# A Mamba mixer on one NeuronCore: product with B to SBUF, scan and product with C in place, convolutions over shifted rows

## The chip, the cores and the metric

The kernel runs on one core of one Trainium2 chip. The metric is the device time of one execution in microseconds. Five engines work side by side, each with its instructions in order: TensorE (PE, with its weight loads PEld), VectorE (DVE), ScalarE (ACT), GpSimd (POOL) and SyncE (SP), which here issues nearly all DMAs. They wait for each other through semaphores.

## The reference, cut to what matters

The input is 8 sequences of 256 tokens with 128 features. A macaron of blocks runs over it; the last three are experts, mixer, experts, each added to the residual stream:

```python
x = x + 0.5 * ffn(layernorm(x)); x = x + attn(layernorm(x)); x = x + 0.5 * ffn(layernorm(x))
x = x + 0.5 * experts(layernorm(x))
x = x + mixer(layernorm(x))
x = x + 0.5 * experts(layernorm(x))
```

Only the mixer is touched. It projects to 256 channels x and 256 gates z, and runs one selective state-space branch forward and one over the reversed sequence:

```python
x = silu(causal_dwconv(x, conv_w, conv_b))            # 4 taps along the tokens
dt, Bm, Cm = split(einsum('bdl,ed->bel', x, xproj_w)) # 64, 16, 16
delta = softplus(dtproj_w @ dt + dt_bias)
dA  = exp(delta * A)                                  # 256 channels x 16 states
dBu = delta * Bm * x
h   = dA * h + dBu                                    # a recurrence over the 256 tokens
y   = (sum over states of h * Cm + D * x) * silu(z)
```

A third branch takes a 2-D FFT of x, a convolution of 5 taps, an inverse FFT and a normalized magnitude. The three are summed and projected back to 128 features.

## The kernel before

The first 1243 us hold the attention blocks and are the same in both kernels. Then `experts_and_mixer` runs. It works on 4 chunks of 512 tokens (two sequences each). The 256 channels x 16 states of a chunk are 32 *units* for the two directions `r`, the two channel halves `t`, four places `i` and two `jp`; a unit is a tile of 128 partitions (8 channels x 16 states) by 2 x 512 tokens. 4 x 32 = 128 units in all.

One loop over *slots* writes the order of TensorE, VectorE, ScalarE and GpSimd by hand (`tc.manual_schedule`); `at(slot, f, ...)` hangs other steps into a slot, ahead of the y-sums or, with `last=True`, behind them. In slot i:

- `scan(i)`: VectorE runs the recurrence (L1217, `tensor_tensor_scan`) over dA (SBUF) and pU (PSUM) into a tile h; then GpSimd multiplies h with C into a second tile hc (L1219).
- `feed(i + 1)`: VectorE multiplies pU by B, in place in PSUM (L1206).
- the steps of the slot; in odd slots `sums(i - 3)`, in which TensorE adds hc over the states into py (L1236).
- `spread(i + 2, m...)`, last in the slot: TensorE copies rows of `du` (delta times u) to the 128 partitions of a unit in pU (two PSUM tiles in turn), and rows of `dl` (delta) to p; ScalarE turns the latter into dA (L1197, L1199). After a *burst* of activation-table work the loop gives out no, one or two new dA a slot.

Steps that the change also touches: `convolve` (L1082) makes one direction of one half with 4 matmuls per output, one a tap, whose 128x128 weights `inK` are the projection times the tap (made on VectorE by `taps`, L872), so that the convolution is taken straight from the normalized features xT. `steps` (L1133) makes delta before the softplus, `delta` (L1153, L1155) adds its two terms on VectorE, multiplies by u on GpSimd and swaps the partition halves of du by two DMAs. `pairs` (L1267), `mirror`, `halves`, `folds` and `squares` are GpSimd's work on the FFT branch, `mix` (L1280), `over_channels` and `over_tokens` (L1312, L1313) TensorE's. `join` (L1416) sums the branches on GpSimd, `output` (L1425) projects, `add` (L1437) adds the residual on GpSimd. Expert tiles (`hidden` L1001 to L1010, `turn` L1019, `close` L1029) run in the slots before the first scan and, for the second block, after the last.

```python
dB = units[n]["dB"]
nc.vector.tensor_tensor(dB, dB, bcast(gots[ch]["B", r], 2), ALU.mult)
...
h = pool.tile([P, 2, CT], F32, tag="h", name="h", bufs=2)
...
nc.vector.tensor_tensor_scan(hf, af, bf, 0.0, ALU.mult, ALU.add)
st["hc"] = hc = pool.tile([P, 2, CT], F32, tag="hc", name="hc", bufs=4)
nc.gpsimd.tensor_tensor(hc, h, bcast(gots[ch]["C", r], 2), ALU.mult)
```

Of the kernel before, what the change touches and what calls it, by code (L numbers as in the profile page):

```python
# [17 lines left out]
P = 128  # L18
B, S, D = 8, 256, 128
CT = 512  # L20
# [795 lines left out]

def experts_and_mixer(nc, tc, ident, nhalf, x, cols, ins, w, given, store):
# [19 lines left out]
    with ExitStack() as ctx:  # L837
        pool = ctx.enter_context(tc.tile_pool(name="mamba", bufs=1))
        ps = psum(ctx, tc)

# [5 lines left out]
        xT = pool.tile([P, 2, S + 6], F32, name="xT")  # L846
        nc.gpsimd.memset(xT[:, :, 0:3], 0.0)
        nc.gpsimd.memset(xT[:, :, S + 3 :], 0.0)
        xTm = xT[:, :, 3 : S + 3]
# [4 lines left out]

        tiny = pool.tile([P, 1], F32, name="tiny")
# [5 lines left out]
        def at(slot, f, *a, last=False):  # L861
            (after if last else before).setdefault(slot, []).append(lambda: f(*a))
# [5 lines left out]

        def taps(r, t):

            to = w["inK"][:, r, t]
            nc.vector.tensor_tensor(to, to, bcast(w["inT"][:, t * P : (t + 1) * P], K), ALU.mult)  # L872
# [81 lines left out]
        class Experts:  # L954
# [39 lines left out]
            def hidden(self, n):  # L994
# [9 lines left out]
                h = pool.tile([P, 2, E, EH], F32, tag="h", name="hid", bufs=2)  # L1004
                gate = got["gate"][:, t : t + 1, :, :].to_broadcast([P, 2, E, EH])
                nc.vector.tensor_tensor(h, ph, gate, ALU.mult)  # L1006
                both = pool.tile([P, 2, 4, P], F32, tag="hc", name="sg_hT", bufs=4)
# [37 lines left out]
        def normalize(ch, part):  # L1045
            got = gots[ch]
            h = part % 2
            xh = x[ch][:, 2 * h : 2 * h + 2, :]
            if part < 2:
                got["stats", h] = ln_scales(nc, pool, nhalf, xh, 1e-5)  # L1050
                return
            if h == 0:
                got["xn"] = given["xT"].rearrange("p (t d) -> p t d", t=NT)
            ln_scaled(nc, xh, got["xn"][:, 2 * h : 2 * h + 2, :], got["stats", h])

        def features(ch):
            pt = bank([P, 2, S])
            for t in range(NT):
                nc.tensor.transpose(
                    pt[:, t // 2, t % 2 * P : (t % 2 + 1) * P], gots[ch]["xn"][:, t, :], ident  # L1060
                )
            nc.scalar.copy(xTm, pt)

        def gate(ch, t):
            got = gots[ch]
            if t == 0:
# [3 lines left out]
                pz, w["inT"][:, DI + t * P : DI + (t + 1) * P], xTm, start=True, stop=True  # L1070
            )
            nc.scalar.copy(got["sz"][:, t, :], pz.rearrange("p b l -> p (b l)"))

        def convolve(ch, t, r):
# [5 lines left out]
            for k in range(K):  # L1080
                o = k if r == 0 else 2 * (K - 1) - k
                nc.tensor.matmul(  # L1082
                    pu, w["inK"][:, r, t, k, :], xT[:, :, o : o + S], start=(k == 0), stop=(k == K - 1)
                )
# [20 lines left out]
        def ranks(ch, r):  # L1105

            got = gots[ch]
            if r == 0:
                got["low"] = pool.tile([LOW, 2, CT], F32, tag="low", name="low")
            px = bank([P, CT])[0:LOW, :]  # L1110
            for t in range(2):
                nc.tensor.matmul(  # L1112
                    px, w["xproj"][:, r, t, :], got["u", t][:, r, :], start=(t == 0), stop=(t == 1)
                )
            nc.scalar.copy(got["low"][:, r, :], px)

        def rows(ch, r, k):
# [4 lines left out]
            n = DR + DS * k  # L1122
# [3 lines left out]
        def steps(ch, t, r):  # L1126

            got = gots[ch]
            if r == 0:
                got["dl", t] = pool.tile([P, 2, CT], F32, tag=f"dl{t}", name=f"dl{t}")  # L1130
                got["ab"] = pool.tile([P, 2, CT], F32, tag="ab", name="ab")
            pd = bank([P, CT])
            nc.tensor.matmul(  # L1133
                pd,
                w["dtT"][:, r, t * P : (t + 1) * P],
                got["low"][0:DR, r, :],
                start=True,
                stop=True,
            )
            b = dt_b[:, r, t : t + 1]  # L1140
            nc.scalar.activation(got["ab"][:, r, :], pd, AF.Abs, bias=b)
            nc.scalar.activation(got["dl", t][:, r, :], pd, AF.Relu, bias=b)
# [6 lines left out]
        def delta(ch, t, part):  # L1149
# [5 lines left out]
            nc.gpsimd.tensor_tensor(ab, dl, u, ALU.mult)  # L1155

            du = pool.tile([P, 2, CT], F32, tag=f"du{t}", name=f"du{t}")
            nc.sync.dma_start(out=du[0:64], in_=ab[64:128])
            nc.sync.dma_start(out=du[64:128], in_=ab[0:64])
            got["du", t] = du  # L1160
# [14 lines left out]
        def spread(n, *ms):  # L1175
# [3 lines left out]
            if 0 <= n < N:  # L1179
                ch, t, r, i, jp = unit(n)  # L1180
                pU = ps.tile([P, 2, CT], F32, tag="u", name="pU")
                for jj in range(2):
                    todo.append((jj, pU[:, jj, :], gots[ch]["du", t][:, r, :], i, 2 * (1 - jp) + jj))
                units[n]["dB"] = pU
            ms = [m for m in ms if 0 <= m < N]
            decays = []
            for k, m in enumerate(ms):
                ch, t, r, i, jp = unit(m)
                dA = pool.tile([P, 2, CT], F32, tag="dA", name="dA", bufs=4)
                units[m]["dA"] = dA  # L1190
                for jj in range(2):
                    pA = bank([P, CT])
                    todo.append((2 * k + jj, pA, gots[ch]["dl", t][:, r, :], i, 2 * jp + jj))
                    decays.append((dA[:, jj, :], pA, A[:, r, t, i, 2 * jp + jj : 2 * jp + jj + 1]))
            for _, dst, src, i, j in sorted(todo, key=lambda v: v[0]):
                rs = slice(32 * j, 32 * j + 32)
                nc.tensor.matmul(dst, w["sel"][rs, i, :], src[rs, :], start=True, stop=True)  # L1197
            for dA, pA, rate in decays:
                nc.scalar.activation(dA, pA, AF.Exp, scale=rate)  # L1199

        def feed(n):
# [3 lines left out]
            dB = units[n]["dB"]  # L1205
            nc.vector.tensor_tensor(dB, dB, bcast(gots[ch]["B", r], 2), ALU.mult)  # L1206

        def scan(n):
# [4 lines left out]
            h = pool.tile([P, 2, CT], F32, tag="h", name="h", bufs=2)  # L1213
            hf, af, bf = (v.rearrange("p t l -> p (t l)") for v in (h, st["dA"], st["dB"]))
            if r == 1:
                hf, af, bf = (v[:, ::-1] for v in (hf, af, bf))
            nc.vector.tensor_tensor_scan(hf, af, bf, 0.0, ALU.mult, ALU.add)  # L1217
            st["hc"] = hc = pool.tile([P, 2, CT], F32, tag="hc", name="hc", bufs=4)
            nc.gpsimd.tensor_tensor(hc, h, bcast(gots[ch]["C", r], 2), ALU.mult)  # L1219

        def skip(ch, t, r):

            got = gots[ch]
            if r == 0:
                got["y", t] = ps.tile([P, CT], F32, tag="y", bufs=1, name="py")
            nc.tensor.matmul(  # L1226
                got["y", t], w["D"][:, 2 * r + t, :], got["u", t][:, r, :], start=(r == 0), stop=False
            )

        def sums(n):  # L1230
# [4 lines left out]
            for j in range(4):  # L1235
# [3 lines left out]
                    units[n + j // 2]["hc"][:, j % 2, :],  # L1239
                    start=False,  # L1240
                    stop=(n % 16 == 14),
                )
            units[n].clear()
# [15 lines left out]
        def pairs(ch, o):  # L1259
# [3 lines left out]
            if o == 1:  # L1263
                got["sd"] = pool.tile([P, 2, 2, 2, 2, M], F32, tag="f8", name="sd", bufs=2)
            lo, hi = (got["xe"][:, :, :, v : v + M] for v in (2 - o, 2 + o))
            for k, op in enumerate((ALU.add, ALU.subtract)):
                nc.gpsimd.tensor_tensor(got["sd"][:, k, o - 1], hi, lo, op)  # L1267
# [146 lines left out]
        def join(ch):  # L1414
            got = gots[ch]
            nc.gpsimd.tensor_tensor(  # L1416
                got["sz"], got["sz"], got["mag"].rearrange("p t b l -> p t (b l)"), ALU.add
            )

        def output(ch):  # L1420
            y = gots[ch]["sz"]
            po = bank([P, NT, D])
            for t in range(NT):
                for d in range(2):
                    nc.tensor.matmul(  # L1425
                        po[:, t, :],
                        y[:, d, t * P : (t + 1) * P],
                        w["outT"][:, d, :],
                        start=(d == 0),
                        stop=(d == 1),  # L1430
                    )
            o = pool.tile([P, NT, D], F32, tag="sq", name="o", bufs=2)
            nc.scalar.copy(o, po)
            gots[ch]["o"] = o

        def add(ch):
            nc.gpsimd.tensor_tensor(x[ch], x[ch], gots[ch]["o"], ALU.add)  # L1437
# [20 lines left out]
        for part, k in enumerate((-20, -18, -19, -17)):  # L1458
            at(k, normalize, 0, part)
        at(-16, features, 0)  # L1460
        for i in range(4):
            at(-15 + i, convolve, 0, 1 - i // 2, i % 2)
        at(-11, gate, 0, 0)
        at(-10, gate, 0, 1)
        at(-9, ranks, 0, 0)
# [4 lines left out]
        at(-13, silu, u_of(0, 1))  # L1470
        at(-11, silu, u_of(0, 0))
        at(-9, silu, sz_of(0))
# [22 lines left out]
        for i in range(4):  # L1495
            at(-23 + i, taps, i // 2, i % 2)
# [14 lines left out]
        bursts = set()  # L1511
        for ch in range(NCH):

            o = (ch - 1) * UNITS
            if ch == 0:
                at(-8, ranks, ch, 1)
                at(-8, largest, ch)
                at(-7, steps, ch, 0, 0)
                at(-6, steps, ch, 0, 1)
                at(-6, exponentials)  # L1520
                at(-6, softplus, ch)
            else:
                for part, k in enumerate((-23, -22, -1, -1)):
                    if ch == 1 and part < 2:
                        k = -6
                    at(o + (0 if ch == 1 and part > 1 else k), normalize, ch, part)
                at(o, features, ch, last=True)
                at(o + 2, convolve, ch, 1, 0)
                at(o + 6, convolve, ch, 1, 1)
                at(o + 8, convolve, ch, 0, 0)  # L1530
                at(o + 10, convolve, ch, 0, 1)
                at(o + 12, silu, u_of(ch, 1), u_of(ch, 0))
                at(o + 12, gate, ch, 0)
                at(o + 12, gate, ch, 1)
                at(o + 12, silu, sz_of(ch))
                at(o + 12, exponentials)
                at(o + 15, ranks, ch, 0)
                at(o + 16, ranks, ch, 1)
                at(o + 17, steps, ch, 0, 0)
# [341 lines left out]
```

## Time and profile before

| | us |
|---|---|
| median of 3 runs (lowest, highest) | 1970.21 (1969.56, 1971.91) |
| the profiled execution | 1971.64 |
| its span, first to last instruction | 1969.9 |
| busy in the span: PE, DVE, ACT, POOL | 1860.1, 1503.3, 1019.3, 1074.3 |
| first scan starts, last scan starts | 1352.8, 1896.9 |
| mean granted TensorE clock | 0.982 |

In the profile's rows a group is named by its source line, engine, operation and tiles (out<-in); after the count stand the busy time in us, the mean of one in ns, the engine's idle time just before these instructions, and what ended most of that. An instruction that has started and is held inside its engine counts as busy. TensorE's matmul times are modelled ends of pipelined work.

### The profile page before, as it was taken

The page shows a single profiled execution, that of the slowest core. Times are in us where ns is not written, and L with a number is a line of the kernel's source. Part 1 is how long each engine was busy: PE and PEld are TensorE (multiplying, and loading weights), DVE is VectorE, ACT ScalarE, POOL GpSimd, SP SyncE. Part 2 cuts the span into 40 slices and gives each one's busy share as a digit, 9 for nine tenths or more (in the row PEclk, how much of TensorE's full clock was granted, in tenths as well). Part 3 has the DMA queues.
Part 4 walks back from the last instruction along what each step waited for, and adds up shares of the span by engine and source line. Part 5 has one row for each costly group of instructions (what it writes and reads, how often), then busy time and mean ns, then how long its engine had stood idle before and what let it go on. Part 6 is the DMA issues. An engine that isn't in the chain of part 4 may idle for free. (4 is left out here: it accounts for less than half of the span.)

```text
span 1969.9 us, 45628 instructions
## 1 busy us (share of the span) xinstructions
PE 1860.1 (94%) x17792; PEld 1143.3 (58%) x17792; DVE 1503.3 (76%) x2573; ACT 1019.3 (52%) x1911; POOL 1074.3 (55%) x1399
## 2 busy tenths in 40 slices
PE   6999999998999999899999999799989999989888
PEld 5777777764565666577777776453344344345345
DVE  5777777787878777577777777647997887997874
ACT  2666666662333222166666666445555654654544
POOL 4333333357666655433333334644878787787864
PEclk9999999998999999899999999999999999999899
DMA  4000000000000000000000000321000010000000
GB/s 151 3 3 3 3 3 3 3 3 1 2 2 2 2 2 2 1 3 3 3 3 4 3 3 3 113 72 26 12 22 22 0 30 15 12 21 12 0 1 22
DMA packets 21242, 29.27 MB, mean 15 GB/s; under 512 B 12506, under 2 KB 13914, under 8 KB 20260
## 3 DMA queue, kind: packets, MB, share of 16 engines
q1 hardware_dynamic: 20740, 26.15, 4.5%
q8 instruction: 142, 2.33, 0.5%
q14 instruction: 72, 0.59, 0.1%
q10 hardware_dynamic: 288, 0.20, 0.0%
HBM read 16.10 MB, written 1.05 MB: 9 GB/s over the span
## 5 line engine op out<-in xcount | busy, mean ns | idle before, releaser
L350 DVE TENSOR_REDUCE negmax<-sc 128x2 f32<-128x512 f32 x768 | 475.0, 677 | 126.7 <-PE sc L342 126.4
L355 ACT ACTIVATE ex<-sc 128x512 f32<-128x512 f32 x768 | 398.0, 603 | 231.9 <-PE sc L342 231.9
L342 PE MATMUL sc<-qk,qk 32*128 32x256 f32 x6144 | 423.1, 397 | 8.0 <-DVE tp L393 2.7
L342 PEld LDWEIGHTS sc<-qk,qk 32*128 32x128 f32 x6144 | 309.8, 187 | 109.7 <-issue 65.5
L1219 POOL TENSOR_TENSOR hc<-h,C 128x1024 f32<-128x1024 f32 x128 | 301.3, 2357 | 112.0 <-DVE h L1217 106.9
L298 POOL TENSOR_SCALAR qk<-qkraw,head_rows,w_bqk 128x256 f32<-128x256 f32 x384 | 207.8, 555 | 203.8 <-ACT qkraw L294 197.8
L1217 DVE TENSOR_TENSOR_SCAN h<-dA,pU 128x1024 f32<-128x1024 f32 x128 | 292.1, 2282 | 13.4 <-POOL hc L1219 0.9
L406 POOL TENSOR_TENSOR cn<-tp,rec 128x256 f32<-128x256 f32 x96 | 59.5, 620 | 287.1 <-DVE rec L404 287.1
L1199 ACT ACTIVATE dA<-p,cols 128x512 f32<-128x512 f32 x256 | 162.1, 684 | 102.8 <-PE p L1197 100.6
L1206 DVE TENSOR_TENSOR pU<-pU,B 128x1024 f32<-128x1024 f32 x128 | 155.7, 1216 | 59.0 <-PE p L1197 51.8
L385 PE MATMUL pc<-ex,va 128*32 128x256 f32 x3072 | 185.7, 382 | 0.3 <-ACT ex L355 0.3
L639 ACT ACTIVATE ex<-sc 128x512 f32<-128x512 f32 x128 | 66.1, 603 | 204.5 <-PE sc L624 204.5
L1197 PE MATMUL pU<-du,s_sel 32*128 32x512 f32 x512 | 146.4, 645 | 19.5 <-DVE h L1217 14.0
L1197 PE MATMUL p<-dl,s_sel 32*128 32x512 f32 x512 | 154.2, 635 | 4.3 <-ACT dA L1199 4.2
L624 PE MATMUL sc<-rot,rot 32*128 32x256 f32 x2048 | 135.2, 388 | 0.3 <-POOL rot L607 0.3
L385 PEld LDWEIGHTS pc<-ex,va 128*32 128x32 f32 x3072 | 90.0, 109 | 78.1 <-ACT ex L355 28.0
L642 POOL TENSOR_TENSOR both<-ex 128x512 f32<-128x512 f32 x64 | 80.0, 1271 | 71.7 <-ACT ex L639 71.7
L624 PEld LDWEIGHTS sc<-rot,rot 32*128 32x128 f32 x2048 | 97.9, 184 | 35.1 <-issue 22.6
L634 DVE TENSOR_REDUCE anegmax<-sc 128x2 f32<-128x512 f32 x128 | 79.4, 683 | 22.1 <-PE sc L624 22.1
L1197 PEld LDWEIGHTS pU<-du,s_sel 32*128 32x128 f32 x512 | 40.3, 185 | 89.6 <-issue 65.2
L393 DVE STREAM_TRANSPOSE tp<-pc 128x512 f32<-128x512 f32 x96 | 68.6, 715 | 28.0 <-PE pc L385 28.0
L1010 POOL TENSOR_TENSOR sg_hT<-sg_hT,hid 128x512 f32<-128x512 f32 x32 | 40.5, 1267 | 65.9 <-ACT sg_hT L1009 65.9
(293 smaller groups left out, 3098.7 us busy)
## 6 DMA issues: line engine op xcount, KB each, us to landing
qk<-turned SPq DMA_DIRECT2D x768, 1.0 KB
s_fft<-s_fft SPq DMA_DIRECT2D x5, 1024.0 KB
du<-ab SPq DMA_DIRECT2D x16, 256.0 KB
B<-low SPq DMA_DIRECT2D x64, 32.0 KB
C<-low SPq DMA_DIRECT2D x64, 32.0 KB
x<-x SPq DMA_DIRECT2D x4, 256.0 KB
s_inK<-s_inK SPq DMA_DIRECT2D x1, 1024.0 KB
out<-x SPq DMA_DIRECT2D x4, 256.0 KB
```

Of the source, the lines that this page charges most:

```text
L298: nc.gpsimd.tensor_scalar(t[:, g, :], raw[:, i, :], w["mask"][:, g : g + 1], w["bqk"][:, c, i, g : g + 1], ALU.mult, ALU.add,)
L342: nc.tensor.matmul(sc[:, t, :], lhs[:, t * P : (t + 1) * P], rhs, start=True, stop=True)
L350: nc.vector.tensor_reduce(sh[:, :, 4 * g + j], sc, AX.X, ALU.max, negate=True)
L355: nc.scalar.activation(ex, sc, AF.Exp, scale=FD**-0.5)
L385: nc.tensor.matmul(st["pc"][32 * j : 32 * j + 32, g, :], st[2][:, kt, 2 * j + g, :], st["ex", g, j][:, kt, :], start=(kt == 0), stop=(kt = ...
L624: nc.tensor.matmul(sc[j][:, t, :], lhs[r, part, t * P : (t + 1) * P] if part < 2 else sel[r, :], rhs[r, part, :] if part < 2 else st["nm"] ...
L642: nc.gpsimd.tensor_tensor(both, ex[:, :, 0], ex[:, :, 1], ALU.add)
L1197: nc.tensor.matmul(dst, w["sel"][rs, i, :], src[rs, :], start=True, stop=True)
L1199: nc.scalar.activation(dA, pA, AF.Exp, scale=rate)
L1206: nc.vector.tensor_tensor(dB, dB, bcast(gots[ch]["B", r], 2), ALU.mult)
L1217: nc.vector.tensor_tensor_scan(hf, af, bf, 0.0, ALU.mult, ALU.add)
L1219: nc.gpsimd.tensor_tensor(hc, h, bcast(gots[ch]["C", r], 2), ALU.mult)
```

## The change

- `feed` writes the product with B into an SBUF tile h; `scan` runs in place over h with dA, and GpSimd multiplies h by C in place. One ring of six h tiles takes the place of two h and four hc tiles; the expert tiles `hid` and `sg_hT` use it too.
- `spread` comes ahead of the slot's other steps (a second dA of a slot goes behind the y-sums), and the order of its matmuls follows which rows they read. `du` is no longer swapped by DMAs.
- The convolution is split: `inputs` projects the features to x, copies it to SBUF, sends it to HBM in four pieces and reads it back four times, shifted by 0 to 3 tokens, into `shifted`; `convolve` then needs four matmuls on 32 output columns each instead of four full ones. `taps` goes.
- `output` takes both branches and the residual (by an identity matmul) into one PSUM sum and ACT writes x; `join` and `add` go.
- `keep_busy` fills slots with little TensorE work with matmuls on a tile of zeros, by a table of estimated work. Over the kernel this makes 49 matmuls of 256 columns.
- Slots of many steps are moved; `pairs` is cut in two, `steps` does both directions at once, `normalize` takes the scales of a chunk's halves together.

```diff
 def convolve(ch, t, r):
-            for k in range(K):
-                o = k if r == 0 else 2 * (K - 1) - k
+            for g in range(4):
                 nc.tensor.matmul(
-                    pu, w["inK"][:, r, t, k, :], xT[:, :, o : o + S], start=(k == 0), stop=(k == K - 1)
+                    pu[32 * g : 32 * g + 32],
+                    w["taps"][:, r, t, g, :],
+                    shifted[:, g, :, 3 * r : 3 * r + S],
+                    start=True,
+                    stop=True,
                 )
+        def inputs(ch, t):
+            px = bank([P, 2, S])
+            xT = gots[ch]["xT"]
+            nc.tensor.matmul(px, w["inT"][:, t * P : (t + 1) * P], xT, start=True, stop=True)
+            xs = pool.tile([P, 2, S], F32, tag="sq", name="xs", bufs=2)
+            nc.scalar.copy(xs, px)
+            there = hbm.tile([32, 4, 2, S], F32, tag="xs", name="xs_rows")
+            for g in range(4):
+                nc.sync.dma_start(out=there[:, g], in_=xs[32 * g : 32 * g + 32])
+            for k in range(K):
+                nc.sync.dma_start(
+                    out=shifted[32 * k : 32 * k + 32, :, :, K - 1 - k : K - 1 - k + S],
+                    in_=there,
+                )
...
 def delta(ch, t, part):
-            nc.gpsimd.tensor_tensor(ab, dl, u, ALU.mult)
-            du = pool.tile([P, 2, CT], F32, tag=f"du{t}", name=f"du{t}")
-            nc.sync.dma_start(out=du[0:64], in_=ab[64:128])
-            nc.sync.dma_start(out=du[64:128], in_=ab[0:64])
-            got["du", t] = du
+            got["du", t] = du = pool.tile([P, 2, CT], F32, tag=f"du{t}", name=f"du{t}")
+            nc.gpsimd.tensor_tensor(du, dl, u, ALU.mult)
...
 def feed(n):
-            dB = units[n]["dB"]
-            nc.vector.tensor_tensor(dB, dB, bcast(gots[ch]["B", r], 2), ALU.mult)
+            units[n]["h"] = h = pool.tile([P, 2, CT], F32, tag="h", name="h", bufs=6)
+            nc.vector.tensor_tensor(h, units[n]["dB"], bcast(gots[ch]["B", r], 2), ALU.mult)
 def scan(n):
-            h = pool.tile([P, 2, CT], F32, tag="h", name="h", bufs=2)
-            hf, af, bf = (v.rearrange("p t l -> p (t l)") for v in (h, st["dA"], st["dB"]))
+            h = st["h"]
+            hf, af = (v.rearrange("p t l -> p (t l)") for v in (h, st["dA"]))
             if r == 1:
-                hf, af, bf = (v[:, ::-1] for v in (hf, af, bf))
-            nc.vector.tensor_tensor_scan(hf, af, bf, 0.0, ALU.mult, ALU.add)
-            st["hc"] = hc = pool.tile([P, 2, CT], F32, tag="hc", name="hc", bufs=4)
-            nc.gpsimd.tensor_tensor(hc, h, bcast(gots[ch]["C", r], 2), ALU.mult)
+                hf, af = (v[:, ::-1] for v in (hf, af))
+            nc.vector.tensor_tensor_scan(hf, af, hf, 0.0, ALU.mult, ALU.add)
+            nc.gpsimd.tensor_tensor(h, h, bcast(gots[ch]["C", r], 2), ALU.mult)
...
+        def keep_busy(k):
+            y = live.get("y")
+            to = bank([P, S]) if k and y is None else y
+            for _ in range(k):
+                nc.tensor.matmul(
+                    to[:, 0:S], zeros, w["G"][:, 0, 0, :], start=y is None, stop=y is None
+                )
...
 def output(ch, h):
+            terms = (got["sz"], got["mag"].rearrange("p t b l -> p t (b l)"))
+            po = bank([P, 2, D])
...
+                nc.tensor.matmul(po[:, i, :], ident, x[ch][:, t, :], start=False, stop=True)
+            nc.scalar.copy(x[ch][:, 2 * h : 2 * h + 2, :], po)
...
-                at(o + 2, convolve, ch, 1, 0)
-                at(o + 6, convolve, ch, 1, 1)
+                at(o + 2, inputs, ch, 1)
+                at(o + 10, inputs, ch, 0)
+                at(o + 6, convolve, ch, 1, 0)
+                at(o + 8, convolve, ch, 1, 1)
...
             for i in range(min(before), max(*before, *after) + 1):
                 scan(i)
                 feed(i + 1)
-                for f in before.get(i, ()):
-                    f()
+                n, some = i + 2, []
+                if i >= -3:
+                    more = 0 if i in bursts or i - 1 in bursts else 2 if i in wide else 1
+                    some = sorted(range(m, m + more), key=lambda v: (v - n + 1) % 2)
+                    m += more
+                spread(n, *some[:1])
+                for f, a in before.get(i, ()):
+                    f(*a)
                 if i % 2:
                     sums(i - 3)
-                for f in after.get(i, ()):
-                    f()
-                more = 0
-                if i >= -4:
-                    more = next(((0, 0, 1, 2, 1, 1, 2)[i - b] for b in bursts if 0 <= i - b < 7), 1)
-                spread(i + 2, *range(m, m + more))
-                m += more
+                spread(None, *some[1:])
+                for f, a in after.get(i, ()):
+                    f(*a)
+                busy = 0.43 * (1 + len(some)) + 0.85 * (i % 2)
+                busy += sum(work.get(f, 0) for f, _ in before.get(i, []) + after.get(i, []))
+                if 0 <= i < N:
+                    keep_busy(max(0, math.ceil((BUSY - busy) / 0.43)))
```

## The prediction, made before the change was run

> **What bounds the kernel now.** I read the page first: the span, the chain and the costliest groups.
>
> ```profile
> span 1969.9 us, 45628 instructions
> ...
> PE pU L1197 5%; DVE h L1217 4%; PE p L1082 3%; PE p L1280 2%; PE p L1197 2%; DVE pU L1206 2%; PE py L1236 2%; PE ph L1001 2%; PE p L1312 1%; POOL hc L1219 1%; PE p L1313 1%; DVE hid L1006 1%; PE p L1029 1%; PE p L1112 1%; PE py L1226 1%
> ...
> L1219 POOL TENSOR_TENSOR hc<-h,C 128x1024 f32<-128x1024 f32 x128 | 301.3, 2357 | 112.0 <-DVE h L1217 106.9
> ...
> L1217 DVE TENSOR_TENSOR_SCAN h<-dA,pU 128x1024 f32<-128x1024 f32 x128 | 292.1, 2282 | 13.4 <-POOL hc L1219 0.9
> ...
> L1206 DVE TENSOR_TENSOR pU<-pU,B 128x1024 f32<-128x1024 f32 x128 | 155.7, 1216 | 59.0 <-PE p L1197 51.8
> ```
>
> Only the mixer is edited. Its 128 scans start between 1352.8 and 1896.9 us, so I cut the end of the span into the stretch before the scans, the stretch of the scans and the tail (columns: length, then busy time and count of each engine).
>
> ```profile
> 1243.00:1352.80 109.80, 96.71 (x412) 56.11 (x413) 54.31 (x155) 57.22 (x96) 51.31 (x69) 0.98 0.28 94
> 1352.80:1899.20 546.40, 506.95 (x2388) 223.53 (x2388) 475.36 (x348) 296.79 (x470) 430.32 (x313) 0.98 0.06 13
> 1899.20:1969.90 70.70, 58.18 (x312) 39.52 (x312) 36.16 (x125) 36.27 (x62) 33.42 (x38) 0.97 0.04 16
> ```
>
> In the scan stretch VectorE is busy 475 of 546 us, TensorE 507, GpSimd 430. One unit costs VectorE a product with B (1.22) and a scan (2.28); POOL's product with C (2.36) runs beside the next unit's work. Undisturbed, scans follow each other every 3.54 us; the mean is 546.4 / 128 = 4.27. VectorE's 71 us of idleness is mostly waiting for spread matmuls (59.0 at L1206), so a lighter and better spread TensorE load could gain up to 71 us. That is the bright side. The dark side is in the timeline of one place in this stretch, VectorE first, then GpSimd (start, length, instruction).
>
> ```profile
> 1378.42 1.21 DVE L1206 TENSOR_TENSOR pU<-pU,B 128x1024 f32<-128x1024 f32 x1
> 1379.54 2.54 DVE L1153 TENSOR_TENSOR dl<-dl,ab 128x1024 f32<-128x1024 f32 x1
> 1382.00 2.27 DVE L1217 TENSOR_TENSOR_SCAN h<-dA,pU 128x1024 f32<-128x1024 f32 x1
> ```
> ```profile
> 1378.65 2.35 POOL L1219 TENSOR_TENSOR hc<-h,C 128x1024 f32<-128x1024 f32 x1 [1.19 <-DVE h L1217]
> 1380.95 3.12 POOL L1267 TENSOR_TENSOR sd<-xe 128x540 f32<-128x540 f32 x2
> ```
>
> The product with B takes pU from PSUM and only B from SBUF: 1.21 us with POOL at work on top of it. The sum dl + ab has both inputs in SBUF: 2.54 us, and it ends at 1382.08, that is 1.08 us after POOL's hc ended at 1381.00. Of POOL's two sd, the one behind it took 2.07 instead of 1.11. The same sum before the scans, with POOL idle, took 1.22. So the two engines excluded each other for whole instructions. Another opcode shows it too (min/median/max):
>
> ```profile
> L807 DVE SCALAR_TENSOR_TENSOR gate<-mark,sc x8: 191/192/1267, 1242.3 to 1951.2; 128x32 f32<-128x32 f32 x8
> ```
>
> Both inputs of L807 are in SBUF; its 1267 ns run ended 50 ns after the 1.27 us POOL instruction that it met.
>
> **The change, part by part.** *Feed and scan.* The product with B now goes from PSUM into an SBUF tile h, and the scan reads dA and h, both SBUF. Today's scan reads one SBUF and one PSUM operand, and runs at 2253 to 2289 ns whatever POOL does. No scan with two SBUF inputs is in the trace, so its price is bounded: 2.29 us if the scan is exempt, or a wait for every POOL instruction that reads SBUF, like L1153. I take the second: operand placement is what separates L1153 and L807 from L1206 and L1217, not the opcode.
>
> The Trainium skill, "SBUF — State Buffer", section "Who interferes with whom", names no exemption: any VectorE instruction with two SBUF inputs contends with a GpSimd instruction that reads SBUF, and the later one is blocked until the first is done. By that rule the sum is the one I take; by the scan's own rows alone it would be the fast rival's.
>
> The sum for the scan stretch, as time in which one engine holds off the other:
> - 128 scans. A waiting L1153 ended 1.08 after POOL instead of running 1.22, so 0.14 of the fixed part is hidden: 2.28 - 0.14 = 2.14 each, 273.9.
> - 128 products with C: 2.357 each, 301.7. Each needs its scan; from scan end (1378.51) to hc start (1378.65) pass 0.14: 17.9.
> - POOL's other work, which queues between the products: 430.3 - 299.0 (hc) = 131.3 in the stretch; less the removed join (3 x 2.36 = 7.1) and residual add (3 x 1.27 = 3.8), less 1.3 of memsets, less 1.0 of sd's waiting: 118.1.
> - seven dl + ab at 1.08: 7.6.
>
> Together 719.2, against 546.4: +172.8. The product with B (1.22) is free: it lies under hc (2.36). From below: without the 17.9 of handovers (POOL has a backlog) and with 0.15 of fixed part hidden in some 90 waiting POOL instructions (14), 687, +141. From above: all 71 us of today's VectorE idleness stays on top, 790, +244. I take 719: the load per unit is then 5.6 us, and TensorE's is 506.95 / 128 = 4.0 before it is lightened, so its waits should go.
>
> *Convolutions.* Four convolutions per chunk shrink from 3.44 us of TensorE (the chain's "PE p L1082 x8") to four column-tiled matmuls. The y-sums L1236 are so tiled: eight records in 0.99. So 4 x 2.45 = 9.8 us less, and two input products (0.86 each, like L1069) more: 8.1 us saved a chunk. Before the scans these lie on the chain; in the scan stretch nobody waits for them any more. In exchange each half-chunk goes out to HBM and back by 8 DMAs on SP's in-order queue, behind which the s_fft fetches and the B and C rows stand. One half-chunk writes 1 MB of shifted rows. The best 18 us of DMA traffic after 1240 us moved 247 GB/s, so 4.2 us at least for the return, perhaps 10 with both hops; convolve stands three slots behind (12 us at the 4 us of that stretch) or four (22 us at 5.6). If that cover failed, TensorE would stop at convolve, with the spreads behind it, for a few us a time. Also four tap products leave VectorE (L872, 0.7 each). For the stretch before the scans: between +3 and -10, I take -5.
>
> *The rest.* The du swap DMAs (16) go, so du is there sooner: nothing waits for it visibly. Steps 0 and 1 run on two row groups; normalize merges two halves: under 2 us a chunk, on POOL, left out. Output takes the residual through an identity matmul and ACT's copy: 16 matmuls more on TensorE, hidden. The zero matmuls of keep_busy, 49 of about 0.43 us, stand at slot ends on TensorE, which now has over 1.5 us of slack a unit; uncovered they would cost 21 us. The shared ring of six h tiles: hid and sg_hT take two a tile and release within two slots, 0. The tail keeps its chain of expert tiles: 0.
>
> Profiled execution: 1971.64 = 1969.9 of span and 1.7 around it. 1971.64 + 172.8 - 5 = 2139.4; the median of the runs stands 1.4 below that execution: **2138 us**, 8.5% slower. Own range: 1970.2 + 141 - 10 = 2101 to 1970.2 + 244 + 3 = 2217, the upper end only if no TensorE wait goes.
>
> **The rivals.** *Faster: the scan is exempt* (its rows never showed a wait). Then VectorE's 475 us is the floor, and between half and all of the 71 idle us go: 1970 - 36 - 8 = 1926, down to 1891. It decides if the scan rows stay near 2.29. Against it: both other opcodes waited. Chance 0.05.
>
> *Half of it:* scans and products alternate, but POOL's other 118 us slip under the products with B. 128 x 4.64 + 7.6 = 601.5: +55 - 5, 2020. Against it: hc already covers that time. Chance 0.06.
>
> *TensorE's clock takes over.* After a window in which TensorE had little to do, its clock is halved (column eight; column two is TensorE's busy time):
>
> ```profile
> 1454.20:1457.60 3.40, 1.58 (x14) 0.63 (x11) 3.27 (x3) 0.94 (x3) 3.40 (x5) 0.99 0.23 51
> 1457.60:1461.00 3.40, 3.40 (x9) 2.39 (x8) 2.09 (x1) 0.60 (x2) 2.50 (x2) 0.50 0.00 0
> ```
>
> At 5.6 us a unit with at most 4.0 of TensorE in it, more windows fall that low. At half clock all along, even 3.3 us a unit (my guess for 4.0 less the lighter convolutions and the waits inside the records) would be 6.6, 845 in all: +299, 2264. Against it: a slow window is a full one, and the slow stretches among today's scans last one or two such windows. The Trainium skill, "TensorE: Matmul & The Clock Gate", Part 1, puts the half rate after an idle window of about 3.4 us; the first window here was busy for 1.58 of 3.40, so the trace goes further, and by the page alone this rival would cost nothing. Chance of over 2200: 0.09.
>
> *The change does nothing that counts* (the freed PSUM buffers and the lighter TensorE, with VectorE as before): 0.01.
>
> **How the numbers follow.** Main case 0.79, of which nearly all lies between 2101 and 2200. The range 2095 to 2200 leaves out the fast rival, the half case and the clock. A measurement of this kernel tells about 0.2% from no change. Faster 0.05, same 0.01, slower 0.94.
>
> **What would show it.** Right: scan rows of about 4.4 us (2.1 of work, 2.3 of wait, counted as busy), VectorE near 95% busy in the stretch, scan starts 4.6 us apart where POOL has only hc and 5.6 in the mean, convolve rows at about 0.9 us, TensorE's busy share down. Wrong: scan rows at 2.29; or starts at 4.6 with long stretches of neither engine waiting; or VectorE idle before the scan for dA or pU, which would put the time on TensorE, ACT or the DMA round trip.

## The result, and the profile after

The changed kernel takes 2124.81 us (median of 4 runs, 2121.70 to 2130.29) against 1971.06 (1969.56 to 1972.72) in the same session: 1.0783 times as long, 95% interval 1.0755 to 1.0811. The profiled execution took 2122.08 us. The page of after, the parts that answer to those of before:

```profile
span 2120.0 us, 46124 instructions
...
L1265 DVE TENSOR_TENSOR_SCAN h<-dA,h 128x1024 f32<-128x1024 f32 x128 | 403.6, 3154 | 59.9 <-ACT dA L1247 51.3
...
L1266 POOL TENSOR_TENSOR h<-h,C 128x1024 f32<-128x1024 f32 x128 | 398.4, 3126 | 38.2 <-DVE h L1265 25.4
...
L1254 DVE TENSOR_TENSOR h<-pU,B 128x1024 f32<-128x1024 f32 x128 | 153.0, 1196 | 22.8 <-PE p L1245 19.7
```

In the mean, scan and product with C both got dearer, by 0.87 and 0.77 us, though their shapes are the same; the product with B kept its price. The three stretches, from the first weight load of the mixer (`s_inT`) to the first scan, to the end of the last scan, and to the end (length, then busy time and count of PE, PEld, DVE, ACT, POOL, then clock, DMA share, GB/s):

```profile
1241.20:1363.10 121.90, 92.49 (x405) 53.30 (x408) 52.39 (x151) 56.93 (x95) 48.46 (x63) 0.86 0.32 94
1363.10:2040.50 677.40, 549.47 (x2580) 246.10 (x2575) 588.23 (x348) 299.59 (x480) 638.37 (x298) 0.90 0.08 17
2040.50:2120.00 79.50, 62.06 (x336) 42.88 (x334) 36.71 (x126) 38.65 (x65) 32.76 (x38) 0.92 0.04 14
```

The prediction cut before's first stretch at 1243.00; its first load is at 1245.3, so this is the stretch that compares:

```profile
1245.30:1352.80 107.50, 95.23 (x408) 55.73 (x411) 54.27 (x154) 57.22 (x96) 49.20 (x67) 0.98 0.29 96
```

Against 107.5, 546.4 and 70.7 after has +14.4, +131.0 and +8.8. That it reaches the mixer 4.1 us earlier is scatter: in the executions that were profiled, the first load lies anywhere between 1241.2 and 1249.5 us. GpSimd, 79% busy in the scan stretch before, is now 94% busy. Of VectorE's 131 us more there, 113 are busy time, nearly all in the scan's rows, and 18 are idle. How GpSimd's time and VectorE's fit together is in the timeline of a steady place, VectorE first, then GpSimd (equal instructions in a row are one line, with their sum):

```profile
1504.62 1.20 DVE L1254 TENSOR_TENSOR h<-pU,B 128x1024 f32<-128x1024 f32 x1
1505.92 3.09 DVE L1265 TENSOR_TENSOR_SCAN h<-dA,h 128x1024 f32<-128x1024 f32 x1
1508.94 1.19 DVE L1254 TENSOR_TENSOR h<-pU,B 128x1024 f32<-128x1024 f32 x1
1510.23 3.08 DVE L1265 TENSOR_TENSOR_SCAN h<-dA,h 128x1024 f32<-128x1024 f32 x1
```
```profile
1502.51 17.23 POOL L1266 TENSOR_TENSOR h<-h,C 128x1024 f32<-128x1024 f32 x4
```

Scan ends are 4.30 us apart (1509.01, 1513.31), and GpSimd's four products take 17.23 / 4 = 4.31 each with no gap: each works about 2.15 and waits, inside its own row, for a scan. A scan's row is 3.09 because VectorE does the product with B (1.20) in the first half of GpSimd's turn: 4.30 - 1.20 = 3.10.

Such places are a part of the stretch: 37 of the 127 distances between scan ends lie from 4.25 to 4.35 us, and the mean is 5.3. Most products with C did not wait (min/median/max ns):

```profile
L1266 POOL TENSOR_TENSOR h<-h,C x128: 2333/2356/4425, 1365.4 to 2043.3; 128x1024 f32<-128x1024 f32 x128
```

51 of them took over 2.45 us. 93 of the 128 scans took over 2.35 us, and 89 of these held on until one GpSimd instruction that reads had ended; in many of these turns it was not a product but other work of GpSimd.

### The profile page after: what moved, and what is told of

The parts are those of the page before. It is cut to its first block, busy times and chain, and to the rows that moved or that the text cites. A ratio compares the mean times of both kernels' runs of the same rounds, so it can differ in the third digit from the quotient of the medians.

```text
span 2120.0 us, 46124 instructions
## 1 busy us (share of the span) xinstructions
PE 1899.6 (90%) x18002; PEld 1164.3 (55%) x18002; DVE 1614.7 (76%) x2569; ACT 1024.3 (48%) x1923; POOL 1281.2 (60%) x1380
## 5 line engine op out<-in xcount | busy, mean ns | idle before, releaser
L1265 DVE TENSOR_TENSOR_SCAN h<-dA,h 128x1024 f32<-128x1024 f32 x128 | 403.6, 3154 | 59.9 <-ACT dA L1247 51.3
L1266 POOL TENSOR_TENSOR h<-h,C 128x1024 f32<-128x1024 f32 x128 | 398.4, 3126 | 38.2 <-DVE h L1265 25.4
L1247 ACT ACTIVATE dA<-p,cols 128x512 f32<-128x512 f32 x256 | 162.5, 684 | 132.4 <-PE p L1245 123.9
L1245 PE MATMUL pU<-du,s_sel 32*128 32x512 f32 x512 | 155.7, 675 | 34.9 <-DVE h L1254 34.9
L1245 PE MATMUL p<-dl,s_sel 32*128 32x512 f32 x512 | 169.6, 681 | 9.4 <-ACT dA L1247 8.7
L1254 DVE TENSOR_TENSOR h<-pU,B 128x1024 f32<-128x1024 f32 x128 | 153.0, 1196 | 22.8 <-PE p L1245 19.7
L1012 DVE TENSOR_TENSOR hid<-ph,gate 128x1024 f32<-128x1024 f32 x32 | 39.1, 1220 | 69.6 <-PE ph L1007 64.2
```

The lines of the kernel that those rows point to most:

```text
L1254: nc.vector.tensor_tensor(h, units[n]["dB"], bcast(gots[ch]["B", r], 2), ALU.mult)
L1265: nc.vector.tensor_tensor_scan(hf, af, hf, 0.0, ALU.mult, ALU.add)
L1266: nc.gpsimd.tensor_tensor(h, h, bcast(gots[ch]["C", r], 2), ALU.mult)
```

## The experiments

The times of all runs, with the stretches of each profiled execution (a single execution, which may lie some us off the median). "Before" had a median of 1971 to 1974 in every session; the ratio is to the runs of that session.

| kernel | median (lowest, highest) | ratio, 95% interval | before scans, scans, tail |
|---|---|---|---|
| before | 1971.06 | 1 | 107.5, 546.4, 70.7 |
| after | 2124.81 | 1.0783 (1.0755, 1.0811) | 121.9, 677.5, 79.5 |
| e1 after, B in PSUM | 2012.73 (2008.34, 2018.21) | 1.0200 (1.0178, 1.0222) | 122.6, 562.7, 77.6 |
| e2 before, ring and in-place alone | 2147.30 (2138.65, 2150.78) | 1.0886 (1.0868, 1.0904) | 107.6, 712.1, 73.4 |
| e3 after, GpSimd only writes | 1979.97 (one run) | | 122.6, 531.4, 75.7 |
| e4 after, no zeros matmuls | 2125.11 (2124.79, 2128.36) | 1.0772 (1.0755, 1.0788) | 119.7, 677.3, 79.5 |
| e5 e1, spreads at the slot's end | 2022.05 (2017.57, 2032.27) | 1.0224 (1.0189, 1.0260) | 124.8, 579.8, 76.7 |
| e6 after, SP in program order | 2120.73 (2117.68, 2126.50) | 1.0735 (1.0700, 1.0770) | 114.6, 683.7, 78.0 |
| e7 before, light convolution | 2004.35 (2001.64, 2010.71) | 1.0147 (1.0114, 1.0180) | 120.4, 561.6, 72.0 |
| e8 the same, loads apart | 1973.52 (1967.26, 1982.41) | 1.0004 (0.9985, 1.0024) | 109.4, 544.4, 77.7 |
| e9 e1, convolution of before | 2016.19 (2013.95, 2020.09) | 1.0215 (1.0184, 1.0246) | 112.2, 582.4, 75.7 |
| e11 after, old rule for dA | 2140.78 (2138.06, 2145.07) | 1.0841 (1.0810, 1.0872) | 124.8, 687.1, 77.3 |
| e12 e1, old rule for dA | 2044.45 (2038.93, 2046.42) | 1.0347 (1.0310, 1.0383) | 128.3, 591.8, 75.1 |
| e13 e9, old rule and swap | 1999.46 (1993.53, 2005.58) | 1.0128 (1.0109, 1.0147) | 118.2, 560.7, 75.4 |

### Is it the scan's second SBUF operand? (e1, e2, e3)

Theory 1: the scan with both inputs in SBUF and GpSimd's reading instructions exclude each other. Theory 2: the scan is as before, and something else of the change costs the time. e1 undoes the part in the changed kernel:

```diff
-            units[n]["h"] = h = pool.tile([P, 2, CT], F32, tag="h", name="h", bufs=6)
-            nc.vector.tensor_tensor(h, units[n]["dB"], bcast(gots[ch]["B", r], 2), ALU.mult)
+            dB = units[n]["dB"]
+            nc.vector.tensor_tensor(dB, dB, bcast(gots[ch]["B", r], 2), ALU.mult)
...
-            nc.vector.tensor_tensor_scan(hf, af, hf, 0.0, ALU.mult, ALU.add)
+            nc.vector.tensor_tensor_scan(hf, af, bf, 0.0, ALU.mult, ALU.add)
```

> The changed kernel with one part undone: the product with B stays in PSUM, in place, and the scan reads dA (SBUF) and pU (PSUM) into h; everything else as changed. Theory 1 (VectorE's scan and GpSimd exclude each other because both scan inputs lie in SBUF): scan rows back at 2.25 to 2.29 us, the scan stretch falls from 677 to 500-545 us (475 us of VectorE work plus some waits), the time to 1945-2000 us. Theory 2 (the new slots, the DMA round trip or TensorE's clock make it slow): the time stays above 2090 us.

Measured: 112 us less than after, but 13 us above the upper end that was expected. e2 makes only this part, in the kernel before (the product with B into a ring of six, scan and product with C in place, as in the change's diff).

> The kernel before with this part alone: the product with B goes to an SBUF tile h, scan and product with C work in place in one ring of six; slots, convolutions, output as before. Theory 1: scan rows from 2.28 to 4.4 us with a mean near 3.1, two scans 4.3 us apart where GpSimd has only the product with C, the scan stretch 650-720 us, the time 2075-2145 us. Theory 2: within 1% of 1971 us.

Measured: +173 us by itself, a little above the range. The scan's rows, of after, then of e1 (min/median/max ns), then two groups in e2's page:

```profile
L1265 DVE TENSOR_TENSOR_SCAN h<-dA,h x128: 2257/3080/9042, 1363.1 to 2036.8; 128x1024 f32<-128x1024 f32 x128
```
```profile
L1265 DVE TENSOR_TENSOR_SCAN h<-dA,pU x128: 2266/2287/2289, 1368.0 to 1928.4; 128x1024 f32<-128x1024 f32 x128
```
```profile
L1217 DVE TENSOR_TENSOR_SCAN h<-dA,h 128x1024 f32<-128x1024 f32 x128 | 385.1, 3009 | 9.7
...
L1206 DVE TENSOR_TENSOR h<-pU,B 128x1024 f32<-128x1024 f32 x128 | 154.1, 1204 | 127.8 <-PE p L1197 111.7
```

With pU as an operand, no scan of 128 waited. Not all of e2's loss lies in the scan's rows: its scan stretch is 166 us longer than before's, of which 94 are busy time of VectorE and 71 idle, most of it at the product with B, which waits 112 us for TensorE's matmuls for p instead of 52. The granted clock of that stretch is 0.86 instead of 0.98; how much of the 71 us the clock carries was not tested.

e3 keeps both operands of the scan in SBUF and takes GpSimd's reads away instead: a memset stands in place of the product with C, which is left out.

```diff
-            nc.gpsimd.tensor_tensor(h, h, bcast(gots[ch]["C", r], 2), ALU.mult)
+            nc.gpsimd.memset(h, 0.001)
```

> The changed kernel with the product with C left out and replaced by a GpSimd memset of the same tile, so GpSimd writes 128x1024 but reads nothing there. If only GpSimd's reads are excluded: scans beside a memset run 2.29 us, waits only behind pairs, folds and the like, the time 1930-2000 us. If any GpSimd work excludes the scan: scan rows keep a median near 3.1 us and the time stays above 2050 us.

Its timeline, VectorE, then GpSimd:

```profile
1427.49 2.29 DVE L1265 TENSOR_TENSOR_SCAN h<-dA,h 128x1024 f32<-128x1024 f32 x1
...
1503.52 4.31 DVE L1265 TENSOR_TENSOR_SCAN h<-dA,h 128x1024 f32<-128x1024 f32 x1
...
1509.05 3.05 DVE L1265 TENSOR_TENSOR_SCAN h<-dA,h 128x1024 f32<-128x1024 f32 x1
```
```profile
1426.53 1.84 POOL L1266 MEMSET h<- 128x1024 f32 x2
...
1503.33 2.35 POOL L1365 TENSOR_TENSOR sp<-fsc 128x1024 f32<-128x1024 f32 x1
...
1508.86 1.09 POOL L1324 TENSOR_TENSOR sd<-xe 128x540 f32<-128x540 f32 x1
```

The median scan is back at 2.29. The scan at 1427.49 started beside a memset that ran until 1428.37, and took 2.29; so it is with all 33 scans that started beside a memset, none of which took over 2.30. Each of the 38 longer scans started beside a GpSimd instruction that reads: the one at 1503.52 ended 2.15 after the reading `sp` did (1505.68). These scans work in place too, so writing over an input is not what makes a scan long. A memset is shorter than a product, so the 145 us by which e3 is below after are not the price of the reads alone; that the scan waits for reads and not for writes is read from the rows. This is what the Trainium skill, "SBUF — State Buffer", section "Who interferes with whom", states of any VectorE instruction with two SBUF inputs, and these runs show it for the scan.

So the part costs +173 alone and +112 in the company of the rest, and the rest costs +39 without it. Together they are 151 and not 212: put on top of e2, the rest even saves 22 us (2147.30 to 2124.81). In after, the product with B waits 20 us for TensorE in the scan stretch, and 112 in e2; which step of the rest brings that was not tested.

### What are the other 39 us? (e4 to e9)

Three suspects can be taken away one by one. e4 sets BUSY = 0, so that no zeros matmul is made; e5 puts e1's spreads back to the slot's end; e6 adds SyncE to the engines that keep the written order (`order = {..., engines.SP}`).

> The changed kernel without the 49 matmuls on zeros. Theory 1: TensorE has slack, so within 8 us of 2125 us either way. Rival (they hold up the clock): the granted clock falls well below the 0.95 of the changed kernel and the time rises by more than 15 us.

> The kernel with the product with B left in PSUM (2013 us), and the spreads put back behind the slot's other steps. Theory: with pU held until its scan, a spread at the head of slot i waits on TensorE for scan i and holds back the rest of the slot; at the end of the slot it waits less. Scan stretch from 563 to 515-545 us, time 1965-1995 us. Rival (the new slots of the other steps cost it): within 8 us of 2013.

> The changed kernel with SP's DMAs issued in the order of the program, so that the shifted rows of the first chunk go ahead of the 1 MB fetches of the FFT weights. Theory (the stretch before the scans is longer because convolve waits 16 us for rows that stand behind a fetch): that wait falls below 8 us, the stretch before the scans from 122 to 108-115 us, the time to 2110-2120 us. Rival (the hop over HBM itself is too long): the wait stays above 13 us and the time within 4 us of 2125.

The zeros matmuls do nothing that can be measured, and the place of the spreads is no gain to give back (e5 is 9 us slower than e1; its expectation failed). e6 hit a real wait. In after, before the scans (waits, then the chain: start, us, what), then the same transfer in e6:

```profile
PE p L1119 <- DMA shifted<-xs_rows: 16.1, 2, 8.8
```
```profile
1291.03 1.25 POOL fw_pairs L924
1292.29 0.36 SPq L910
...
1292.82 0.66 SPq L1107
...
1294.82 7.66 DMA shifted<-xs_rows
```
```profile
1296.94 6.07 DMA shifted<-xs_rows
```

SyncE put a 1 MB `s_fft` fetch (L910) ahead of the shifted rows. The fetch itself waited for a GpSimd instruction (`fw_pairs`, to 1292.28), and the loads of the rows stood behind it; the rows came 7.66 us after the last of these was issued. In e6 they are issued ahead of the fetch and come after 6.07 us. The wait is 8.5 us instead of 16.1, and the stretch before the scans 114.6 instead of 121.9. Of these 7.3 us, 4 are left in the medians, and the runs of the two kernels overlap; e6 lies just outside what was expected in both wait and time. In its profiled execution, 6 us over its median, the scan stretch is 6 longer, so where the rest went is open.

e7 and e8 ask for the price of the light convolution in the kernel before. In e7, `inputs` of both halves send and load at once, at slots o + 1 and o + 2; there the convolution of half 1 reads the rows that were loaded for half 0. In e8 a half's rows are loaded only behind the other half's convolutions:

```diff
-                at(o + 1, inputs, ch, 1)
-                at(o + 2, inputs, ch, 0)
+                at(o + 1, inputs, ch, 1)
+                at(o + 1, load, ch, 1)
+                at(o + 2, inputs, ch, 0)
+                at(o + 5, load, ch, 0, last=True)
```

> The kernel before with the light convolutions alone (inputs, shifted rows, four matmuls on 32 columns; SP in program order; gates moved up by nine slots), scan and products as before. Theory: 8 us less TensorE work per chunk in the slots where the scans wait for spreads: scan stretch from 546 to 505-535 us, the stretch before the scans within 8 us of 108, time 1930-1965 us. Rival (the waits only move, or the DMA round trip eats it): 1965 us or more.

> The kernel before with the light convolution alone, the shifted rows of one half loaded only when the other half's convolutions have read them (the sends to HBM stay early). Theory 1 (TensorE, in order, stands behind the round trip through HBM, and its clock falls): 1985 to 2015 us, scans at 2.25 to 2.29, 'PE p L1102 <- DMA shifted' still among the waits of the scan stretch and before it. Rival (the loss in the kernel with the light convolution alone came from the two loads standing together in SP's queue): 1940 to 1975, with that wait gone.

e7 took 2004 where 1930 to 1965 was expected, and I believed that the round trip through HBM and the lower clock make the light convolution cost 30 us. e8 refutes it. TensorE's waits for `shifted`, 11.6 us before the scans and 17.5 among them in e7, are 3.2 and none, and the kernel is at the time of before. The light convolution brings nothing and costs nothing by itself; what e7 lost, 31 us, hangs on when its rows are sent and loaded (e8 also has half 1's convolutions one and two slots earlier, which was not taken apart). e9 says the same from the other side: e1 with the four full matmuls put back.

> The changed kernel with the product with B back in PSUM and the convolution back as four full matmuls from the features, so that of the change stay the ring of six, the place of the spreads, the missing du swap, output's sum in PSUM, the zeros matmuls and the moved slots. Theory (the light convolution carries some 30 of the 39 us by which the kernel with B in PSUM is above before): 1970 to 1995 us, the stretch before the scans at 108 to 114. Rival (the moved slots and the order of the spreads carry it): 2005 or more. If these parts bring what TensorE saves: under 1966.

Its rival held: 2016. So the 39 us are in what e9 keeps of the change: the moved slots, the spreads without the swap, the ring with products in place, the sum in `output`. (It keeps the zeros matmuls too, which cost nothing in e4.)

### Which rows the spreads read (e9's trace, e11, e12, e13)

In e9 VectorE stands idle before its scans for 68 us, 56.3 of them for dA (13.4 in all in before). One such place, VectorE, ScalarE and TensorE of e9 (scan L1247, dA L1229, spread L1227):

```profile
1438.04 2.29 DVE L1247 TENSOR_TENSOR_SCAN h<-dA,pU 128x1024 f32<-128x1024 f32 x1 [2.63 <-ACT dA L1229]
...
1443.00 2.29 DVE L1247 TENSOR_TENSOR_SCAN h<-dA,pU 128x1024 f32<-128x1024 f32 x1 [0.96 <-ACT dA L1229]
```
```profile
1441.65 1.26 ACT L1229 ACTIVATE dA<-p,cols 128x512 f32<-128x512 f32 x2 [1.46 <-PE p L1227]
```
```profile
1440.48 0.66 PE L1227 MATMUL pU<-du,s_sel 32*128 32x512 f32 x1 [0.91 <-DVE h L1247]
```

The scan ends at 1440.33; only then is its pU free for the next spread (1440.48), whose matmuls for dl are mixed with those for du; ScalarE's two dA follow (to 1442.91), then the scan (1443.00). The loop takes 4.96 us, and runs of such distances, 4.9 to 5.0 between scan ends, stand behind most bursts in e1, e5 and e9; before has no two in a row. The changed rule gives out dA three units ahead and, after a burst, one; the old rule four and two. So e11 and e12 put the old rule into after and into e1:

```diff
-                if i >= -3:
-                    more = 0 if i in bursts or i - 1 in bursts else 2 if i in wide else 1
+                if i >= -4:
+                    more = next(((0, 0, 1, 2, 1, 1, 2)[i - b] for b in bursts if 0 <= i - b < 7), 1)
```

> The changed kernel with the rule of before for how many new dA a slot gives out (start one slot earlier, 0, 0, 1, 2, 1, 1, 2 after a burst), so that a dA is made four units ahead instead of three, and two instead of one after a burst. Theory A (this rule makes the scans wait for dA, 51 us at the scans of the changed kernel, but there the spread does not wait for the scan, and each pair of scan and product with C holds its 4.29 us anyway): 2095 to 2120 us, with the wait of the scan for dA down to a third. Rival (the rule costs nothing or is needed because the banks fill): 2120 to 2150.

> The changed kernel with the product with B in PSUM (2013 us) and the rule of before for new dA. Theory A (the moved rule is what costs the rest of the change its 39 us: the dA of the next unit stands on TensorE behind the pU matmuls that wait for the scan before it, which makes scans 4.9 to 5.0 us apart after a burst): 1960 to 1985 us, the scan stretch at 525 to 545, the wait of the scan for dA down from 53 us to under 20, and the runs of 4.9 to 5.0 between scan ends gone. If the lighter TensorE then comes through, it beats the kernel before. Rival (some other moved step): 2000 or more.

Both got slower, by 16 and 32 us, as their rivals said. The wait of the scans for dA did fall, from 51.3 to 5.9 us in e11 and from 54.1 to 4.3 in e12, but in e12 the product with B now waited 64.6 us for spread matmuls, 58.2 of them for those of pU (e1: 12.5, nearly all for those of dl). TensorE of e1, then of e12:

```profile
1506.71 0.66 PE L1245 MATMUL pU<-du,s_sel 32*128 32x512 f32 x1 [0.28 <-DVE h L1265]
1506.71 0.69 PE L1245 MATMUL p<-dl,s_sel 32*128 32x512 f32 x1
...
1507.26 0.59 PE L1245 MATMUL p<-dl,s_sel 32*128 32x512 f32 x1
```
```profile
1504.09 1.13 PE L1245 MATMUL pU<-du,s_sel 32*128 32x512 f32 x4
1505.06 1.02 PE L1245 MATMUL p<-dl,s_sel 32*128 32x512 f32 x4
```

In e1 all eight are done in 1.14 us; in e12 the four for du and the four for dl follow each other, 1.99 us. A unit reads 64 of the 128 rows of du or dl, even units the one half, odd units the other. The Trainium skill, "TensorE: Matmul & The Clock Gate", "Part 3: Packing small matmuls", says that matmuls on different groups of 32 rows run at the same time; these rows show it, and what the same rows cost. pU is made two units ahead of the scan. Before, du's halves were swapped by the DMAs, so that pU of unit i + 2 and dA of unit i + 4 read different rows. Without the swap this needs an odd distance, so dA can be made three units ahead, or one, but not four or two. The time in which at least one spread matmul ran, summed over the scan stretch of each trace, is 189 us in before, 175 in e1, 172 in e9 and 186 in after, but 245 in e12 and 254 in e11. e13 puts both back into e9, the swap and the old rule:

```diff
-            nc.gpsimd.tensor_tensor(du, dl, u, ALU.mult)
+            nc.gpsimd.tensor_tensor(ab, dl, u, ALU.mult)
+            nc.sync.dma_start(out=du[0:64], in_=ab[64:128])
+            nc.sync.dma_start(out=du[64:128], in_=ab[0:64])
```

> The changed kernel with the product with B in PSUM and the convolution of before (2016 us), and with two things of before besides: du's halves swapped by two DMAs, and its rule for new dA, four units ahead. Theory B (without the swap, spread matmuls for du and dl use the same 32 rows unless the dA made is an odd number of units ahead of pU, so the change could only lead by three, or by one after a burst; with lead one, dA stands on TensorE behind pU matmuls that wait for the scan): 1965 to 1990 us, scan stretch 540 to 555, spread matmuls covering some 190 us of it (175 with odd lead, 245 in the kernel with the old rule and no swap), the scan's wait for dA under 20 us. Rival (other moved steps make the 43 us): 2000 or more. Under 1966 would beat the kernel before.

Measured: 1999.46, 17 us below e9. The idle time before the scans is 13 us as in before, no longer 68, with spread matmuls at 183 us, and no two distances of 4.9 to 5.0 stand in a row. The swap without the old rule was not run, so the 17 us are the price of the pair. The expected range was missed by 9 us, and 1999.46 stands at the edge of the rival's 2000. The pair explains some 17 of the 44 us that e9 lies above before; what is left, 25 us in e13, lies in the other parts that e9 keeps and was not taken apart (in its profiled execution, 6 us over its median, the stretch before the scans is 11 longer than before's, the scan stretch 14, the tail 5). None of these kernels is faster than before.

## Why the prediction was right, and where not

**Sign and cause: right.** The operand, not the opcode, decides: e1 against after, e2 alone, and the rows of e3. The sum stands in the scan stretch, as said.

**GpSimd's side of the sum: right. The scans' side: too large.** In the trace of after, GpSimd's rows cover 638 us of the scan stretch. 112 of its instructions, 51 of them products with C, took over 0.15 us more than the shortest row of their kind, 218 us together; counted as waiting for VectorE, that leaves 420 us of GpSimd's own work, against 301.7 + 118.1 = 419.8 in the sum. The rest of the stretch is these 218 us and 39 in which GpSimd was idle, 257 together; the sum had 273.9 + 17.9 + 7.6 = 299.4 there. These 42 us are the whole miss.

The steady place shows where such a difference can come from. The sum took 2.14 for a scan, 2.357 for the product with C and 0.14 for the handover, 4.64; the trace has 4.30. I had seen one waiting instruction lose 0.14 of its fixed part, and booked that for VectorE; for GpSimd's instructions, and for the handovers, I took it off in the bound from below alone. Here both engines wait inside the instruction, the product loses its fixed part too (2.36 to 2.15), and no handover is left, because the next instruction has started before the other one ends. But only 37 of 127 distances are of this kind. That 128 x 4.30 + 118.1 + 7.6 = 676 also comes near the measured 677.4 is therefore luck.

**Before the scans: wrong sign.** -5 was forecast, +14.4 came. I let TensorE's saving count and called the round trip covered, with the queue named but its order not looked up: a 1 MB fetch went ahead (e6, 7 us). e9 and e13, without any round trip, are still 5 and 11 us above before's 107.5, which was not explained.

**The tail: 0 forecast, +8.8.** The kernels that keep the moved slots have 75 to 80 us against 70.7, and e2, with the ring part alone, 73.4. That would put most of it on the moved slots, but e8, with before's tail of steps, has 77.7 in an execution 8 us over its median; the cause stays open.

**"The du swap DMAs go: nothing waits for it visibly".** The step that failed most instructively. The swap was no transfer to be saved but what let the spreads of pU and of dA four units ahead share TensorE, and its price, with the rule for dA that hung on it, was 17 us (e9 to e13). In after itself it was not measured apart; e11 shows only that the old rule without the swap is worse.

**The misses nearly cancel.** The scan stretch grew by 42 us less than the sum, the two others by 28 more (19.4 and 8.8), and the execution reached the mixer 4.1 earlier: 2139.4 - 41.8 + 28.2 - 4.1 = 2121.7, against 2122.1 measured. That 2138 came within 14 us of 2124.81 is in part luck.

**The signs to look for.** Scan rows of 4.4 were forecast, 3.08 is the median: I forgot that the product with B fills VectorE for 1.2 of GpSimd's 2.15. VectorE was busy 588 of 677 us, 87% and not 95%: 51 us it waited for dA, one of the signs of being wrong, though a small one. The mean distance of scans is 677.4 / 128 = 5.3, not 5.6. The zeros matmuls were hidden, as said (e4); the residual in `output` was not tested apart.

**The rivals.** An exempt scan is excluded by the rows. So is the half case: 61 of the 112 waiting GpSimd instructions were not products with C, so its other work took turns with the scans too. The clock did fall (0.90 over the scan stretch, 0.98 before), but with TensorE busy 549 of 677 us it stayed short of being the bound; what the lower clock cost was not measured.

## What to carry to other kernels

Before moving a VectorE operand from PSUM to SBUF to free a bank, look at what GpSimd does meanwhile: if it reads SBUF most of the time, the two engines' times can add up, as they did here: 4.30 us a pair in the steady place. Before deleting a copy that only rearranges rows, ask which row groups it lets run together, and what distance between producer and consumer the schedule takes from that. And the order in an in-order DMA queue belongs to the price of every transfer put there: 7 us before the scans in after (e6), and 31 us between e7 and e8 went with the places of sends and loads.

## What the runs showed of the hardware

An engine that is held off is not always served next. In after, 89 of the 93 scans that waited (over 2.35 us) went ahead once one reading GpSimd instruction had ended, three held on through two, and one, of 9.04 us, through three (VectorE, then GpSimd):

```profile
1526.01 9.04 DVE L1265 TENSOR_TENSOR_SCAN h<-dA,h 128x1024 f32<-128x1024 f32 x1 [7.29 <-ACT dA L1247]
```
```profile
1525.83 2.40 POOL L1365 TENSOR_TENSOR sp<-fsc 128x1024 f32<-128x1024 f32 x1
1528.19 2.34 POOL L1266 TENSOR_TENSOR h<-h,C 128x1024 f32<-128x1024 f32 x1
1530.50 2.40 POOL L1365 TENSOR_TENSOR sp<-fsc 128x1024 f32<-128x1024 f32 x1
```

GpSimd's next instruction was ready each time, and the scan ended 2.15 after the last of them (1532.90). In the steady place GpSimd's next product was ready as well and the scan still came first; what decides was not found. e4, whose longest scan took 4.44 us, needs the same 677 us for that stretch, so this is no cost of its own. What I had also not expected is that two engines that exclude each other can lose no time between turns: 4.30 a pair in the steady place, against 2.28 + 2.36 = 4.64 for the two alone.
